# Products of zeros at the head of a conditional-residual kernel, and other planned times for its prologue

## The chip, the cores and the metric

The kernel runs on one core of a Trainium2 chip. A core has TensorE (PE in the profile; its weight loads are PEld), VectorE (DVE), ScalarE (ACT), GpSimd (POOL) and SyncE (SP), each with its own queue of instructions, and 16 DMA engines that move data between HBM and on-chip memory. All tensors are f32. The metric is the device time of one execution in microseconds, as the median of three runs.

## The reference

Four residual layers follow each other on x of shape (8, 512, 256), each with the condition cond of shape (8, 256):

```python
x = x + L0(x, cond)   # mixture of experts: a shared expert of 512, and 2 of 8 routed experts of 128
x = x + L1(x, cond)   # Haar analysis and synthesis with a gate made from cond, plus its input
x = x + L2(x, cond)   # low-rank layer; its rank-8 factors are generated from cond by W2
x = x + L3(x, cond)   # GRU over the 512 positions, then a projection
```

L0 computes `silu(x @ sw1.T) * (x @ sw3.T)` times sw2 for the shared expert, and for each routed expert `gelu(x @ rw1[e].T)` times rw2[e], weighted by gates from a sigmoid, the two best of eight scores, and a normalisation; the sum is divided by 3. L1's scales share one gate per channel, so that the layer comes down to a factor per channel and batch. L2 normalises cond, makes a hidden vector from it, and from that and W2 (8 MB) the matrices a1, b1, a2, b2. L3 takes 512 steps one after the other:

```python
Z = sigmoid(xz + H @ Whz.T + bhz);  R = sigmoid(xr + H @ Whr.T + bhr)
H = Z * H + (1 - Z) * tanh(xh + R * H @ Whh.T + bhh);  Y = H @ Whq.T + bhq
```

## The kernel before

Time is cut into 16 windows of 32 positions; a window holds 8 x 32 = 256 columns (NT). L0 to L2 of a window are matmuls of 256 columns; they run ahead of the recurrence, which then takes the window's 32 steps. Nearly all of these products go through `quads` (L485), which issues four matmuls side by side, each into its own 32 output partitions. The names of the tiles in the profile: hp and low hold hidden activations of the experts, acc their sum over experts, misc several small products, grh and gz the recurrence's gates. sw_sb, rw_sb, wsq_a and w are weights; x is the input (and, early, memory lent to pieces of W2).

Before the first step of the recurrence lies a prologue. SP's queue loads, in this order, window 0's x in two halves alternating with the two halves of sw13 (both under `load_sw13`), the rest of the first four windows' x, sw2, rw1, the square matrices, rw2, eight pieces of W2, the recurrence's weights wx and wh, and the rest of x. ACT's queue loads cond, the router and small vectors. POOL's queue loads h0 and bias rows, and fetches the broadcast gates bc from a DRAM buffer comb_d. Some engines also do the following small work: mean and variance of cond (`mean_over_features`, L833, with inv_c as stationary operand), the router's bias from cond (`time_bias`, L874), routing of four windows (`route`, L912), dense layers on cond (`dense_cond`, L1034), and the generation of the low-rank matrices (`generate`, L1104).

At the very start, DVE sets a tile `zeros`, and TensorE clears two PSUM banks with it (`claim`, L303): 8 matmuls of 256 columns for each bank. One is gz, which holds the z gate's sums.

The order of instructions is written out by hand, in two ways. In the prologue a planner, `Jobs.run`, keeps a clock for each engine. Every job has an engine, jobs that it depends on, and a planned duration `takes`; the planner goes forward in steps of 0.02 planned us, and where an engine's clock is past, emits the first job in its queue that is ready by plan. `TAKES` holds the planned defaults per engine; `load` computes `takes` of a transfer from its size in MB over RATE. These numbers produce no instruction: they only decide which job is emitted next on each engine. The jobs of windows 0 and 1 are made with the default for TensorE PE_ALONE, all later ones with PE_WOVEN. The prologue's planner stops when window 0's L0, the low-rank matrices and the recurrence's weights are there, and again once the first half of window 0 has passed L2. What of window 1 has been emitted by then is done ahead of the recurrence; the rest is woven into its steps.

In the recurrence the loop writes out each step, and `first_slot` and `second_slot` decide how many jobs of later windows are put into the step's gaps on TensorE, by how far the count of TensorE jobs left lies behind a straight line.

Of the kernel before, what the change touches and what calls it, by code (L numbers as in the profile page):

```python
# [26 lines left out]
NT = B * WS  # L27
# [4 lines left out]
NQ = 4  # L32
# [27 lines left out]
TAKES = {"PE": 0.43, "ACT": 0.4, "DVE": 0.4, "POOL": 0.8, "SP": 0.5}  # L60
PE_ALONE, PE_WOVEN = 0.43, 0.65
LEAD = 20
AHEAD = 1
RATE = 0.36
LAG = 3.5
# [72 lines left out]
class Jobs:  # L138
# [42 lines left out]
    def run(self, until):  # L181

        while any(j.done is None for j in until):
            for eng, at in self.clock.items():
                if at <= self.now:
                    qs = (self.queues[eng], self.small[eng])
                    ready = ((j, q) for q in qs for j in q if j.ready(self.now))
                    job, q = next(ready, (None, None))
                    if job is not None:
                        q.remove(job)  # L190
                        job.emit(self.now)
                        self.clock[eng] = self.now + job.takes
            self.now += 0.02

    def drain(self, now=0.0):
# [8 lines left out]
def cond_resid_kernel(  # L204
# [29 lines left out]
    nc = tc.nc  # L234
# [16 lines left out]
        for e in earlier:  # L251
            tc.declare_no_dep(later.ins, e.ins, reason="through another engine")

    TAKES["PE"] = PE_ALONE
    ctx.enter_context(tc.manual_schedule())
    const = ctx.enter_context(tc.tile_pool(name="const", bufs=1))
    dram = ctx.enter_context(tc.tile_pool(name="dram", bufs=1, space=DRAM))
# [30 lines left out]
    gz = ps_z.tile([P, 2, NG, FQ], F32, name="gz")  # L288
# [6 lines left out]
    zeros = const.tile([P, NT], F32, name="zeros")  # L295
# [3 lines left out]
    def claim(bank):  # L299

        for half in range(2):
            for j in range(NQ):
                nc.tensor.matmul(  # L303
                    bank[ts(j, 32), ts(half, NT)],
                    zeros[:, 0:32],
                    zeros,
                    start=half == 0,
                    stop=half == 1,
                    skip_group_check=True,
                )  # L310

    claim(gz.rearrange("p c n f -> p (c n f)"))
    claim(rh0)

    jobs = Jobs()
    jobs.clock["PE"] = 3.5

    def load(out, in_, mb, lazies=(), eng="SP"):

        issue = {"SP": nc.sync, "ACT": nc.scalar, "POOL": nc.gpsimd}[eng].dma_start  # L320
        return jobs.add(
            eng,
            lambda: issue(out=out.get() if isinstance(out, Lazy) else out, in_=in_),
            (),
            lazies,
            max(1.0 if eng == "POOL" else 0.45, mb / RATE),
            lag=LAG,
        )
# [46 lines left out]
    sw13_sb = const.tile([P, KC, 2, HS], F32, name="sw13_sb")  # L375
    got_sw13 = []

    def load_sw13(k):
        rows = sw13[:, ts(k, P), :].rearrange("g p h -> p g h")
        got_sw13.append(load(sw13_sb[:, k], rows, 0.5))  # L380


    load_x(0, 0.6, (0, 1), load_sw13)
    load_x(0, 0.5, (1, EARLY))
    got_vec = load(vec, vecs, 0, eng="ACT")
# [428 lines left out]
    def pe(fn, deps, lazies=(), takes=0.3):  # L814
        return jobs.add("PE", fn, deps, lazies, takes)

    def dve(fn, deps, lazies=(), takes=0.25):
        return jobs.add("DVE", fn, deps, lazies, takes)
# [4 lines left out]
    def flat(z):  # L823
        t = z.get()
        return t if len(t.shape) == 2 else t.rearrange("p a b -> p (a b)")


    def mean_over_features(src, dep):
        ps = Lazy(r_c)

        def products():
            for k in range(KC):
                nc.tensor.matmul(  # L833
                    ps.get()[:, :B], inv_c, src[:, k, :], start=(k == 0), stop=(k == KC - 1)
                )

        return ps, pe(products, [dep], [ps], 0.9)

    mu, j = mean_over_features(cond, got_cond)
    diff = set1.tile([P, KC, B], F32, name="diff")  # L840

    def center():
        for k in range(KC):
            tt(diff[:, k, :], cond[:, k, :], mu.get()[:, :B], ALU.subtract)

    j = dve(center, [j], [mu], 0.4)
    dsq = set1.tile([P, KC, B], F32, name="dsq")
    j = dve(lambda: tt(dsq, diff, diff, ALU.mult), [j])
    var_ps, j = mean_over_features(dsq, j)
    var = set1.tile([P, B], F32, name="var")  # L850
    j = dve(
        lambda: nc.vector.tensor_scalar(var, var_ps.get()[:, :B], EPS_LN, None, ALU.add),
        [j],
        [var_ps],
    )
# [5 lines left out]
    j = dve(  # L861
        lambda: tt(
            prod,
            rout[:, 1].rearrange("p k (o e) -> p k o e", o=1).broadcast_to([P, KC, B, E]),
            cond.rearrange("p k (b o) -> p k b o", o=1).broadcast_to([P, KC, B, E]),
            ALU.mult,
        ),
        [got_cond, got_rout],
    )
# [12 lines left out]
    j = pe(time_bias, [j], [tb_ps])  # L882
# [140 lines left out]
    def dense_cond(w, src, bias, name, dep):  # L1023

        ps = Lazy(r_c)
        pre = set1.tile([P, KC, B], F32, name=f"{name}_pre")

        def out(m):
            return ps.get()[:, m * B : (m + 1) * B]

        def products():
            for m in range(KC):
                for k in range(KC):
                    nc.tensor.matmul(  # L1034
                        out(m),
                        wsq_a[:, k, w, ts(m, P)],
                        src[:, k, :],
                        start=(k == 0),
                        stop=(k == KC - 1),
                    )  # L1040

        def add_bias():
            for m in range(KC):
                nc.vector.tensor_scalar(
                    pre[:, m, :], out(m), vec[:, bias, m : m + 1], None, ALU.add
                )

        j = pe(products, [dep, got_sq_a], [ps], 0.95)
        return pre, dve(add_bias, [j, got_vec], [ps], 0.4)

    def gated(pre, func, scale, name, dep):
        a = set1.tile([P, KC, B], F32, name=name)
        return a, act(lambda: nc.scalar.activation(a, pre, func, scale=scale), [dep])


    hid_pre, j = dense_cond(A_L2W1, lnc, V_BIAS1, "hid", got_lnc)
    hid_e, j = gated(hid_pre, AF.Erf, RSQRT2, "hid_e", j)
# [10 lines left out]
    g1_pre, j = dense_cond(A_L1W1, cond, V_B1, "g1", got_cond)  # L1068
    g1, j = gated(g1_pre, AF.Sigmoid, 1.0, "g1", j)
    j = dve(lambda: tt(g1, g1, g1_pre, ALU.mult), [j])  # L1070
    gate_pre, j = dense_cond(A_L1W2, g1, V_B2, "gate", j)
    gate, j = gated(gate_pre, AF.Sigmoid, 1.0, "gate", j)
# [8 lines left out]
    for n, of in enumerate(LOW):  # L1081
# [14 lines left out]
        j = pe(biased_rows, [got_b2, got_sq_a], [gp], 0.45)  # L1096
        for k in range(KC):
            got = [pieces[q, k] for q in of]

            def generate(k=k, of=of, gp=gp):  # L1100
# [12 lines left out]
            j = pe(  # L1113
                generate,
                [j, got_hid, *(g[1] for g in got)],
                [gp, *(g[0] for g in got)],
                1.75,
            )
        j = got_low_out[n] = dve(
            lambda n=n, gp=gp: nc.vector.tensor_copy(low_out[:, n], flat(gp)[:, :C]),  # L1120
            [j],
            [gp],
            0.45,
        )
# [8 lines left out]
        j = pe(turn, [j], [lt], 0.6)  # L1133
# [11 lines left out]
    l0_ends = []  # L1145

    ends = [window_jobs(w, routed, xts[w], True) for w in range(2)]
    TAKES["PE"] = PE_WOVEN

    routes = [routed]  # L1150
    for w in range(2, NW):
# [16 lines left out]
    with (  # L1168
# [145 lines left out]
        jobs.run(ends[0][0])  # L1314
        jobs.run(jobs.queues["PE"][:AHEAD])
        base = jobs.now
# [11 lines left out]
        def behind(s, by=0):  # L1328
            return (
                any(j.done is None for j in ends[1][0])  # L1330
                or jobs.left("PE") > all_left * (LAST - s) / (LAST + LEAD) + by
            )
# [29 lines left out]
        for c in range(NTC):  # L1362
            hist = hists[c]
            gates = upcoming
            for t in range(TC):
                s = c * TC + t
                n, u = t // GS, t % GS
# [194 lines left out]
```

## Time and profile before

| | us |
|---|---|
| median of three runs | 1318.25 |
| the runs | 1317.85, 1318.25, 1321.23 |
| the profiled execution | 1318.28 |
| its span, from first to last instruction | 1316.5 |
| TensorE busy | 1178.3 |
| DVE busy | 916.8 |
| ACT busy | 505.7 |
| POOL busy | 150.6 |

Busy time is the union of an engine's instructions in the span. The profile's rows give an instruction's source line, engine, operation, output and inputs; DMA-issuing instructions stand under the queue that issues them (SPq, ACTq, POOLq) and are not counted as busy. A matmul in f32 leaves two records. Idle time before an instruction stands in brackets with what ended it; it is inferred from semaphores, and where an instruction waits for several, the latest event is named. Numbers in the profile refer to the source lines of the kernel before.

### The profile page before, as it was taken

Reading aid. Unit: us, or ns where it says so; the run is one execution under the profiler, and the core shown is the slowest. Engines: PE = TensorE matmul, PEld = TensorE weight load, DVE = VectorE, ACT = ScalarE, POOL = GpSimd, SP = SyncE. Lnnn points to the kernel's source line nnn. Section 1 sums busy time; section 2 is a strip of 40 time slices with the busy share of each in tenths; the row PEclk is TensorE's granted clock in tenths of the full one; section 3 lists DMA queues with packets and bytes.
Section 4 is the critical chain, followed back from the end, with each engine's and each line's share of the span. In section 5 each row is a group of like instructions: output and inputs, shape, how many; then the busy total and the mean of one; then the engine's idle time right before and its main releaser. Section 6 shows DMA issues by size and latency. Waiting matters only on the chain.

```text
span 1316.5 us, 88999 instructions
## 1 busy us (share of the span) xinstructions
PE 1178.3 (89%) x39240; PEld 688.4 (52%) x39240; DVE 916.8 (70%) x6271; ACT 505.7 (38%) x3407; POOL 150.6 (11%) x235
## 2 busy tenths in 40 slices
PE   8999999899999999998888988888888888878886
PEld 5666555555555555555554555545554545545443
DVE  5367777777776767676776767677676767667775
ACT  2134343444344444334343433443434344433332
POOL 3311110101011110101011010101101011110000
PEclk9999999999999999999999999999999999999999
DMA  9910001200010010100000010000001000000111
GB/s 318 352 53 16 5 4 38 52 5 29 13 36 20 12 29 5 52 4 28 12 15 26 4 36 4 22 19 12 28 4 29 12 4 4 4 4 4 36 30 26
DMA packets 41859, 46.46 MB, mean 35 GB/s; under 512 B 27488, under 2 KB 31104, under 8 KB 40320
## 3 DMA queue, kind: packets, MB, share of 16 engines
q1 hardware_dynamic: 38576, 38.31, 9.5%
q8 instruction: 306, 5.01, 1.6%
q0 software_dynamic: 1184, 2.31, 0.5%
q14 instruction: 81, 0.66, 0.2%
q10 hardware_dynamic: 1712, 0.16, 0.1%
HBM read 36.45 MB, written 4.33 MB: 31 GB/s over the span
## 4 chain that ended last, share of the span: by engine, by line
PE 66%; DVE 19%; ACT 9%; issue 4%; DMA 2%; SPq 0%; ACTq 0%
PE grh L1197 35%; PE hp L485 11%; DVE d L1393 7%; DVE rT L1393 6%; PE acc L485 6%; PE gz L1197 5%; ACT c L1379 5%; PE low L485 4%; ACT r L1379 4%; PE misc L485 3%; DVE s_h L1469 3%; DVE s_rh L1410 2%; DMA bc<-comb_d 1%; DMA sw_sb<-in_sw_dram 0%; PE misc L1104 0%
## 5 line engine op out<-in xcount | busy, mean ns | idle before, releaser
L1393 DVE STREAM_TRANSPOSE rT<-r 128x32 f32<-128x32 f32 x1024 | 156.1, 191 | 219.5 <-ACT r L1379 215.8
L1379 ACT ACTIVATE r<-grh 128x32 f32<-128x32 f32 x1024 | 146.3, 195 | 421.0 <-PE grh L1197 418.2
L1197 PE MATMUL grh<-wh,s_h 128*32 128x64 f32 x8192 | 221.8, 225 | 90.1 <-DVE s_h L1469 89.1
L1197 PEld LDWEIGHTS grh<-wh,s_h 128*32 128x32 f32 x8192 | 140.4, 109 | 309.6 <-DVE s_h L1469 308.4
L1379 ACT ACTIVATE c<-grh 128x32 f32<-128x32 f32 x1024 | 146.2, 195 | 313.6 <-PE grh L1197 313.1
L1197 PE MATMUL grh<-wh,s_rh 128*32 128x64 f32 x8192 | 221.6, 225 | 34.3 <-DVE s_rh L1410 10.0
L1197 PEld LDWEIGHTS grh<-wh,s_rh 128*32 128x32 f32 x8192 | 139.2, 108 | 191.8 <-DVE s_rh L1410 188.1
L1393 DVE STREAM_TRANSPOSE d<-c 128x32 f32<-128x32 f32 x1024 | 156.5, 192 | 115.2 <-ACT c L1379 108.9
L1197 PE MATMUL gz<-wh,s_h 128*32 128x64 f32 x8192 | 209.9, 219 | 0.4 <-issue 0.3
L1197 PEld LDWEIGHTS gz<-wh,s_h 128*32 128x32 f32 x8192 | 153.5, 110 | 0.9 <-issue 0.8
L485 PE MATMUL acc<-g,rw_sb 128*32 128x256 f32 x2048 | 153.5, 379 | 0.0
L485 PE MATMUL hp<-x,sw_sb 128*32 128x256 f32 x2016 | 150.8, 384 | 2.6 <-ACT sig L583 2.2
L634 POOL TENSOR_TENSOR g<-gl,bc 128x256 f32<-128x256 f32 x128 | 93.6, 733 | 511.9 <-DVE s_h L1469 358.8
L485 PE MATMUL hp<-x,rw_sb 128*32 128x256 f32 x2016 | 151.4, 380 | 0.7 <-ACT sig L617 0.6
L1469 DVE TENSOR_TENSOR_SCAN s_h<-d,d 128x16 f32<-128x16 f32 x1024 | 145.4, 184 | 0.0
L1410 DVE TENSOR_TENSOR s_rh<-rT,s_h 128x8 f32<-128x8 f32 x1024 | 133.5, 168 | 0.0
L1393 DVE STREAM_TRANSPOSE zT<-z 128x64 f32<-128x64 f32 x512 | 121.9, 238 | 0.4 <-ACT z L1379 0.3
L1379 ACT ACTIVATE z<-gz 128x64 f32<-128x64 f32 x512 | 121.4, 237 | 0.8 <-PE gz L1197 0.4
L1483 ACT COPY hist<-s_h 128x16 f32<-128x16 f32 x512 | 106.3, 208 | 0.5 <-DVE s_h L1469 0.5
L1197 PE MATMUL grh<-wx,xt 128*32 128x128 f32 x2048 | 104.8, 274 | 1.3 <-ACT r L1379 1.1
L1422 DVE TENSOR_TENSOR d<-zT,s_h 128x16 f32<-128x16 f32 x512 | 90.7, 177 | 17.5
L1423 DVE TENSOR_SCALAR d<-zT 128x16 f32<-128x16 f32 x512 | 86.8, 169 | 0.0
(154 smaller groups left out, 1208.7 us busy)
## 6 DMA issues: line engine op xcount, KB each, us to landing
bc<-comb_d SPq DMA_DIRECT2D x56, 256.0 KB, 3.2
w<-in_w_dram SPq DMA_DIRECT2D x5, 1024.0 KB, 13.5
out_dram<-x SPq DMA_DIRECT2D x14, 256.0 KB, 3.2
x<-in_w_dram SPq DMA_DIRECT2D x3, 1024.0 KB, 15.6
x<-in_xT_dram SPq DMA_DIRECT2D x2, 1536.0 KB
bc<-comb_d POOLq DMA_DIRECT2D x8, 256.0 KB, 9.0
sw_sb<-in_sw_dram SPq DMA_DIRECT2D x3, 512.0 KB, 8.0
wsq_a<-in_sq_a_dram SPq DMA_DIRECT2D x1, 1280.0 KB
```

Source lines behind the costliest of these rows:

```text
L485: nc.tensor.matmul(out[ts(j, 32)], lhs[:, ts(j, 32)], rhs, start=start, stop=False, skip_group_check=True,)
L634: lambda gl=gl, g=g, e=e: nc.gpsimd.tensor_tensor(g.get(), gl.get(), bcs[e // 2].get()[:, e % 2], ALU.mult),
L1197: nc.tensor.matmul(out[ts(j, 32)], lhs, rhs[:, ..., ts(j, FQ)], start=start, stop=False, skip_group_check=True,)
L1379: nc.scalar.activation(x, y, func)
L1393: ins = nc.vector.transpose(dst.rearrange("p i u b -> p i (u b)"), src.rearrange("p (i r) -> p i r", r=32),)
L1410: prod = tt(s_rh[u][:, k, u, :], rT[:, k, u, :], h[:, k], ALU.mult)
L1422: tt(d1[:, :, u, :, 1], zT[:, :, u, :], h, ALU.mult)
L1423: nc.vector.tensor_scalar(d0[:, :, :, 1], zT[:, :, u, :], -1.0, 1.0, ALU.mult, ALU.add)
L1469: new = nc.vector.tensor_tensor_scan(s_h[v][:, k, v].rearrange("p b w -> p (b w)"), d0[:, k].rearrange("p b w -> p (b w)"), d1[:, k, u].re ...
L1483: nc.scalar.copy(hist[:, :, t, :], s_h[v][:, :, v, :, 1])
```

## The change

A constant `WARM` of 10.0 planned us is added. While a planned clock is below it, and TensorE's clock is past with no ready job, the planner calls `self.idle()`, which emits four matmuls of zeros, 128 columns wide, into gz (with start and stop off, so they add to the bank that `claim` cleared), and advances TensorE's clock by its default. `add_zeros` takes the place of that call. The planned default of DVE in the prologue becomes 0.45, and goes back to 0.4 when window 1's jobs have been made; each half of sw13 is planned as 0.55 MB in place of 0.5. One added line sets TensorE's clock to 4.0, and the line behind it, which was there, sets it to 3.5.

```diff
+WARM = 10.0
@@ Jobs.run
                         job.emit(self.now)
                         self.clock[eng] = self.now + job.takes
+                    elif eng == "PE" and self.now < WARM:
+                        self.idle()
+                        self.clock[eng] = self.now + TAKES[eng]
@@ cond_resid_kernel
-    TAKES["PE"] = PE_ALONE
+    TAKES["PE"], TAKES["DVE"] = PE_ALONE, 0.45
...
+    def add_zeros():
+        for j in range(NQ):
+            nc.tensor.matmul(
+                gz.rearrange("p c n f -> p (c n f)")[ts(j, 32), : NT // 2],
+                zeros[:, 0:32],
+                zeros[:, : NT // 2],
+                start=False,
+                stop=False,
+                skip_group_check=True,
+            )
...
     jobs = Jobs()
+    jobs.idle = add_zeros
+
+    jobs.clock["PE"] = 4.0
     jobs.clock["PE"] = 3.5
...
-        got_sw13.append(load(sw13_sb[:, k], rows, 0.5))
+        got_sw13.append(load(sw13_sb[:, k], rows, 0.55))
...
     ends = [window_jobs(w, routed, xts[w], True) for w in range(2)]
-    TAKES["PE"] = PE_WOVEN
+    TAKES["PE"], TAKES["DVE"] = PE_WOVEN, 0.4
```

## The prediction

> **What bounds the kernel now.** I read the page first, for the whole; then TensorE's instructions in order of time through the prologue; then narrow stretches; then the waits.
>
> ```profile
> span 1316.5 us, 88999 instructions
> PE 1178.3 (89%) x39240; PEld 688.4 (52%) x39240; DVE 916.8 (70%) x6271; ACT 505.7 (38%) x3407; POOL 150.6 (11%) x235
> ...
> PE 66%; DVE 19%; ACT 9%; issue 4%; DMA 2%; SPq 0%; ACTq 0%
> ```
>
> Two stages make the span. The recurrence of 512 steps begins with its first product of the state, at 67.16 us below, and takes the rest, 1316.5 - 67.2 = 1249.3 us, 2.44 us a step. The scans (L1469) stand at 40 to 42 pairs in every 100 us, with three groups of woven products in half of the steps (early) or a fifth of them (late): the step's own chain of products, gates and transposes sets its pace. So what the change can move is when that first product starts.
>
> ```profile
> 1.19 1.94 PE L303 MATMUL gz<-zeros 128*32 128x256 f32 x16 [1.19 <-DVE zeros L296]
> 2.90 1.93 PE L303 MATMUL grh<-zeros 128*32 128x256 f32 x16
> 4.76 1.02 PE L833 MATMUL grh<-cond,inv_c 128*128 128x8 f32 x4
> 6.12 1.12 PE L874 MATMUL grh<-prod,ones 128*128 128x64 f32 x4 [0.33 <-DVE diff L844]
> 7.60 1.08 PE L485 MATMUL hp<-x,sw_sb 128*32 128x256 f32 x8 [0.36 <-DMA sw_sb<-in_sw_dram]
> 8.61 1.02 PE L833 MATMUL grh<-dsq,inv_c 128*128 128x8 f32 x4
> 9.56 2.79 PE L485 MATMUL hp<-x,sw_sb 128*32 128x256 f32 x24
> ...
> 16.68 0.64 PE L485 MATMUL low<-x,sw_sb 128*32 128x256 f32 x8 [0.51 <-ACT sig L583]
> 17.13 1.05 PE L912 MATMUL grh<-x,rout_sq 128*32 128x256 f32 x16
> 17.99 0.61 PE L485 MATMUL hp<-x,sw_sb 128*32 128x256 f32 x8
> 18.43 1.05 PE L485 MATMUL acc<-g,sw_sb 128*32 128x256 f32 x16
> ...
> 67.16 0.43 PE L1197 MATMUL grh<-wh,s_h 128*32 128x64 f32 x16
> ```
>
> These are TensorE's instructions in time (start, length, count of records; a matmul leaves two records, and four matmuls side by side, eight records, are one "group"). Idle time stands in brackets. From 7.60 us to the loop TensorE idles a few times, by 0.2 to 1.1 us each: the prologue is bound by TensorE's work, and DMA keeps just ahead of it. Now the same kind of group at two speeds, in stretches of 1 us (length, busy and records, granted clock, DMA share, GB/s):
>
> ```profile
> 12.00:13.00 1.00, 1.00 (x16) 1.00 1.02 320
> 13.00:14.00 1.00, 1.00 (x16) 1.00 1.16 399
> 14.00:15.00 1.00, 1.00 (x25) 1.00 1.13 344
> ```
>
> Sixteen records fit into 1 us until 14 us, and 25 after: a group costs 0.86 us before and 0.43 us after (17.99 to 18.43 above). In quarter microseconds the turn lies at about 13.9 us. The column of the granted clock says 1.00 throughout, so this slow state is read from the records' pace alone. From 7.60 to 13.9 TensorE works 6.3 us at half speed, and a fast one would need 3.15 us.
>
> **The head under the change.** Built, the new program holds three calls of add_zeros: four matmuls of 128 columns after the claims, eight between the mean (L833) and the variance product (L833, of dsq). No others: later the planner always finds work. Half as many columns as the claims' groups (0.86 us each, slow) make an estimated 0.43 us a call. Slow throughout, the head runs: claims to 4.8, zeros to 5.25, mean (1.0 us as in its row) to 6.25, zeros to 7.1. The variance product, formerly behind the first group of hp, stands ahead of it and takes to 8.05, 0.45 us of it past the 7.60 at which hp could start; the time-bias product (L874), formerly hidden before 7.6, stands among the hp groups. Work ahead of the first data costs nothing: it lies beside the transfer of sw_sb that ends at 7.46. If that transfer were early, it would cost up to the 1.3 us of the three calls.
>
> **Does it open the clock?** The row: slow from 1.19 to 13.9. [...]
>
> **Sum with the clock open at 7.1.** Variance product: four records, at the fast price of 0.12 us each (L1034's eight records of 128x8 take 0.99 us), to 7.6. Two groups of hp 0.86, time bias 0.5, four groups 1.72: 10.7. The second half of sw_sb was issued at 2.78 and landed 8.0 us later, 10.8, so no wait of note. Six groups 2.6, one group of hp and the routing pair (L912) 1.3: 14.7. In before the same work ends at 18.43. Lead 3.7 us: 3.2 of clock and the 0.51 us that low waited for ACT at 16.68, which the new order (n=0 and n=1 back to back) doesn't wait.
> With the clock shut: 8.05, two groups 1.72, time bias 1.0, 3.6 slow groups to 13.9, then fast: 18.0; lead 0.4.
>
> **Behind the head.** VectorE's planned 0.45 and the load's 0.55 only move instructions (takes is no instruction). No queue of SP or POOL changes its order, and no DMA is added. On TensorE two stalls of 0.57 us on ACT's reads of a bank go (16.68, counted, and 20.90), and two of 0.56 come: hp_5 and hp_8 now have their last group straight behind the group that ACT reads, where a dense product and L1104 stood. Net +0.55. Two more groups of window 1 stand ahead of the loop (one hp of rw_sb, one acc), 0.86 us on TensorE's path, with two fewer in it. There they lay in the step's slack; from steps of (half of three groups) 2.43 and (a fifth) 2.40 us a group costs about 0.1, so the relief is 0.2. Net +0.65. The positions of some tens of other groups in the loop shift by a step; counts of steps with one, two and three groups agree within a few, so 0, at most 0.5 either way.
> Transfers: with TensorE 3 us earlier, each product moved must still find its data. L1104 at 35.09 needs a piece landed at 30.1 (issued 13.5, 16.6 to land), slack 5; at 46.73 one landed at 40.6, slack 6; the fifth w piece waits for TensorE itself and follows it:
>
> ```profile
> SPq L323 <- PE misc L1104: 8.0, 1, 8.0
> SPq L323 <- DMA wsq_a<-in_sq_a_dram: 7.2, 1, 7.2
> ...
> POOL g L634 <- DMA bc<-comb_d: 5.9, 2, 4.5
> ```
>
> SP's own row says when wsq_a landed: 22.36, where SP goes on; its first use at 26.13 moves to about 23. bc lands at 40.9, and its product on POOL (0.73) is wanted at 43.20: slack 1.5, unless routing, VectorE's chain and the comb_d transfer, which all start from L912, move along, as they should. I allow 0.3 for these (bounds 0 and 2.2: all slack lost). First gate of the loop: ACT's idle of 2.8 us is named after bc, but the built instruction waits only for pieces and comb_d writes landed earlier and for the product at 67.16; 0.1 us is all it is late.
> Sum: -3.7 + 0.55 + 0.65 + 0.3 = -2.2. From the profiled execution's 1318.28 (span 1316.5 and 1.8 around it): **1316.1**.
>
> **Rivals.**
> [...]
> The clock opens and the transfers eat it: bc's landing stays at 40.9 because it shares the DMA engines (busy 0.95 or more from 10 to 50 us) with w pieces, so the first rw acc stays at 41.65 at the earliest, 1.5 us before the old one; -1.5 + 1.2 = -0.3, and with wsq_a or sw2 late none: 1318.0. For it: L634's 4.5 us wait. Against: bc was issued only at 34.2, after comb_d.
> The loop's changed order decides, by its few displaced groups or an instruction fetch such as the 1.2 us of "issue" before 70.53: +-0.5 ordinarily, and over 4 us only if it repeated in several steps, which the equal counts don't suggest.
>
> **How the numbers follow.** 0.3% is 3.95 us, about what a measurement of this kernel can tell from no change (the three runs spread 0.26%). Clock open, full gain 0.50 (1316.1, own range 1314.3 to 1317.6); open but eaten 0.20 (1318.0); shut 0.20 (1319.1, 1318.3 to 1320.3); the loop's order 0.10, half either way (1313 or 1323). Faster by 0.3% needs 1314.3: a tenth of the first, a few of the others, and half of the last: 0.14. Slower needs 1322.2: half of the last and tails: 0.09. Range from the first's low tail to the third's high: 1313.9 to 1320.5.
>
> **What would show it.** Right: groups of hp at 0.43 us from about 7.6; L912 near 14; the rw acc near 40; first product of the state near 65; 1249 us after it. Wrong: 0.86 us groups to 13 or 14; TensorE idle before L1104, L1034 or acc with a DMA or POOL named; a start unmoved; or a start moved with a longer loop.

## The result, and the profile after

The changed kernel took 1322.19 us (median of 11 runs, 1318.40 to 1326.02), the kernel before 1318.25 (11 runs, 1316.79 to 1321.31): 1.0025 of it, interval 1.0015 to 1.0035. The forecast was 1316.1 within 1313.9 to 1320.5, so it was wrong in sign and outside its range. The profiled execution took 1324.59 us, 2.4 above the median, while that of before (1318.28) lies at its median: what follows splits the 6 us between these two executions, not the 3.9 between the medians. Its page begins so (span; busy time of each engine; shares of the chain that ended last; one row of the DMA queues):

```profile
span 1322.5 us, 89028 instructions
PE 1181.6 (89%) x39264; PEld 690.8 (52%) x39264; DVE 917.5 (69%) x6271; ACT 505.7 (38%) x3407; POOL 150.5 (11%) x235
...
q8 instruction: 306, 5.01, 1.5%
...
PE 67%; DVE 19%; ACT 9%; issue 4%; ACTq 0%; DVEq 0%
```

TensorE has 24 records more than before (39,264 against 39,240): the 12 matmuls of zeros. The row of queue 8 was not used in the prediction and matters below: 306 packets, 5.01 MB, so 16.4 KB each; TensorE's 39,264 + 39,264 records over 306 packets are 257 a packet.

TensorE in order of time, after (start, length, records; idle time in brackets):

```profile
4.61 0.66 PE L321 MATMUL gz<-zeros 128*32 128x128 f32 x8
5.20 1.02 PE L852 MATMUL grh<-cond,inv_c 128*128 128x8 f32 x4
6.15 1.08 PE L321 MATMUL gz<-zeros 128*32 128x128 f32 x16
7.16 1.02 PE L852 MATMUL grh<-dsq,inv_c 128*128 128x8 f32 x4
8.12 1.94 PE L504 MATMUL hp<-x,sw_sb 128*32 128x256 f32 x16
9.98 1.12 PE L893 MATMUL grh<-prod,ones 128*128 128x64 f32 x4
...
17.20 1.04 PE L931 MATMUL grh<-x,rout_sq 128*32 128x256 f32 x16
18.06 0.61 PE L504 MATMUL hp<-x,sw_sb 128*32 128x256 f32 x8
...
68.70 0.22 PE L1216 MATMUL grh<-wh,s_h 128*32 128x64 f32 x1
...
72.28 0.80 PE L504 MATMUL low<-x,wsq_a 128*32 128x128 f32 x9 [2.61 <-issue]
72.71 0.68 PE L1216 MATMUL grh<-wh,s_rh 128*32 128x64 f32 x15
```

The zeros stand where they were expected and hp starts at 8.12, but its groups still cost 0.86 us: the array stayed slow. The same stretches as shown of before say the same (16 records in 1 us until 14 us):

```profile
12.00:13.00 1.00, 1.00 (x16) 1.00 1.02 323
13.00:14.00 1.00, 1.00 (x16) 1.00 1.06 373
14.00:15.00 1.00, 1.00 (x24) 1.00 1.08 324
```

So the routing product stands at 17.20 (17.13 before), and the first product of the state at 68.70 (67.16), 1.54 us late. Then comes a wait of 2.61 us of a kind that the page calls "issue": TensorE waits for nothing that the profile shows. ScalarE's activation of z, once a step, counts the loop. Before, and then after, the first two:

```profile
67.94 0.23 ACT L1379 ACTIVATE z<-gz 128x64 f32<-128x64 f32 x1
71.78 0.24 ACT L1379 ACTIVATE z<-gz 128x64 f32<-128x64 f32 x1
```

```profile
69.59 0.23 ACT L1398 ACTIVATE z<-gz 128x64 f32<-128x64 f32 x1
75.85 0.24 ACT L1398 ACTIVATE z<-gz 128x64 f32<-128x64 f32 x1
```

The step between them takes 3.84 us before and 6.26 after; an undisturbed one takes 2.42 in both. The last z is 6.00 us later than in before, of which 1.65 are there at the first z, 2.42 come in this step, and 1.93 in the other 510. The tail is the same. TensorE's "issue" waits from 62 us on (total, times, longest), before and after:

```profile
PE low L485 <- issue: 1.2, 1, 1.2
PE grh L1197 <- issue: 1.1, 2, 0.9
PE gz L1197 <- issue: 0.3, 1, 0.3
```

```profile
PE low L504 <- issue: 2.6, 1, 2.6
PE gz L1216 <- issue: 2.2, 5, 0.8
PE hp L504 <- issue: 0.4, 1, 0.4
PE grh L1216 <- issue: 0.2, 1, 0.2
```

They are 2.6 us before and 5.4 after. The 1.20 that the prediction passed over as a possible instruction fetch is the first of them.

### The profile page after: what moved, and what is told of

It is laid out like the page before. It is cut to its first block, busy times and chain, and to the rows that moved or that the text cites. A ratio compares the mean times of both kernels' runs of the same rounds, so it can differ in the third digit from the quotient of the medians.

```text
span 1322.5 us, 89028 instructions
## 1 busy us (share of the span) xinstructions
PE 1181.6 (89%) x39264; PEld 690.8 (52%) x39264; DVE 917.5 (69%) x6271; ACT 505.7 (38%) x3407; POOL 150.5 (11%) x235
## 3 DMA queue, kind: packets, MB, share of 16 engines
q8 instruction: 306, 5.01, 1.5%
## 4 chain that ended last, share of the span: by engine, by line
PE 67%; DVE 19%; ACT 9%; issue 4%; ACTq 0%; DVEq 0%
PE grh L1216 35%; PE hp L504 11%; DVE d L1412 7%; DVE rT L1412 6%; PE acc L504 6%; PE gz L1216 5%; ACT c L1398 5%; PE low L504 5%; ACT r L1398 4%; PE misc L504 4%; DVE s_h L1488 3%; DVE s_rh L1429 2%; PE misc L1123 1%; ACT sig L602 0%; PE grh L1053 0%
## 6 DMA issues: line engine op xcount, KB each, us to landing
x<-in_w_dram SPq DMA_DIRECT2D x3, 1024.0 KB, 14.7
```

## What the waits are

Three readings of the two traces suggested it. First, the place. Counted from the start of the kernel, this gap stands behind the same record of TensorE, the 1111th, in both traces, although the changed program has other instructions there: in before the end of step 0's second woven product, in after the middle of its first, 40 records earlier in the program. The other gaps stand 127 records ahead of it or nearly whole multiples of 128 behind it (a few records are missing from the traces). With 257 records of TensorE a packet, near 128 matmuls and 128 weight loads, I take the place for the end of a block of instructions which one packet of queue 8 brings.

Second, the time of the packet. In the trace's record of queue 8 the packet for this block starts at 68.08 us before and at 69.99 after, and TensorE goes on 2.45 and 2.29 us later. Elsewhere in the loop it mostly starts while 80 to 120 records of the block ahead are still to come (about eight packets in ten), here with 31 left (before) and none (after).

Third, what it waits behind. In stretches of 1 us, the last of 2 us (length, TensorE's busy time and records, granted clock, DMA share, GB/s), before and then after:

```profile
66.00:67.00 1.00, 0.83 (x40) 1.00 1.04 398
67.00:68.00 1.00, 1.00 (x67) 1.00 0.88 338
68.00:69.00 1.00, 0.78 (x39) 1.00 0.34 121
69.00:70.00 1.00, 0.33 (x13) 1.00 0.04 14
```

```profile
67.00:68.00 1.00, 1.00 (x49) 1.00 1.06 405
68.00:69.00 1.00, 1.00 (x63) 1.00 0.89 340
69.00:70.00 1.00, 0.67 (x39) 1.00 0.39 141
70.00:71.00 1.00, 0.00 (x0) 1.00 0.12 45
...
72.00:74.00 2.00, 1.72 (x43) 0.50 0.03 8
```

The last load of x (3 MB for windows 4 to 15) keeps the DMA engines full until about 68 and 69, and the packet of instructions starts as it ends. The last row shows the price on top: after 2.6 us without work the clock was granted at 0.50, and about 3 us of work ran at half speed (until about 75.3).

The theory to test was then: the change's loss comes from where these blocks end, not from the zeros' work or the order. Its 12 matmuls make TensorE's stream 48 instructions longer ahead of the loop, and its two groups more ahead of the loop add to that until the loop, which holds two groups fewer, has evened them out. Every block in the loop then ends at another place in a step and is fetched at another time. Rivals: the zeros' own work at the head; the order that the new planned times give; the bulk load alone.

## Experiments

In the tables "stream" is the count of TensorE's matmuls against the kernel before. Each set shares its chip and its runs of the kernel before.

**The parts of the change, one by one.**

e1_idle_alone: the calls of zeros alone, with the planned times of before.

```diff
-    TAKES["PE"], TAKES["DVE"] = PE_ALONE, 0.45
+    TAKES["PE"], TAKES["DVE"] = PE_ALONE, 0.4
...
-        got_sw13.append(load(sw13_sb[:, k], rows, 0.55))
+        got_sw13.append(load(sw13_sb[:, k], rows, 0.5))
```

> The kernel before plus the calls of add_zeros alone (planned 0.4 for VectorE and 0.5 MB for sw13 kept): the three calls of zeros and the new order at the head, but no extra groups ahead of the loop. Theory A (TensorE runs out of fetched instructions at the loop's start while bulk loads hold the DMA engines, and the clock doesn't open earlier): clock opens at about 13.9 us as before, first product of the state within 0.6 us of the 67.2 of before, but the end of the fetched block lies 24 records earlier in the program, so the stall after step 0 is about 2 us instead of 1.2: 0.5 to 2.5 us slower than before. Theory B (the two extra groups and stalls ahead of the loop make the loss, zeros cost nothing): within 0.5 us of before. Theory C (zeros open the clock in most runs and only the profiled run of the changed kernel missed it): 2 to 3 us faster.

e2_dve_alone: VectorE's planned 0.45 alone, no zeros, the load at 0.5.

```diff
-WARM = 10.0
+WARM = 0.0
...
-        got_sw13.append(load(sw13_sb[:, k], rows, 0.55))
+        got_sw13.append(load(sw13_sb[:, k], rows, 0.5))
```

> The kernel before with VectorE planned at 0.45 in the prologue alone: no zeros, two more groups of window 1 ahead of the loop. Theory A: the loop starts 0.9 to 1.4 us later than in before, the block's end lies 16 records earlier and the bulk loads end later, so the stall grows too: 1.5 to 3.5 us slower. Theory B: 1 to 1.5 us slower, with the stall unchanged at 1.2 us. Theory C: 0.5 to 1.5 us slower.

e3_no_zeros: the order of the changed kernel; a call of idle emits nothing.

```diff
-    jobs.idle = add_zeros
+    jobs.idle = lambda: None
```

> The changed kernel with add_zeros emitting nothing while the planner counts its time: same order as the changed kernel, without the 12 matmuls of zeros. Theory A: the clock opens at the same edge as with them, near 13.9; the block's end moves 24 records later than in the changed kernel, so the stall at the loop's start shrinks from 2.6 us towards 1.5: 1 to 2.5 us faster than the changed kernel's 1322.2, that is 1319.7 to 1321.2. Theory B: within 0.5 us of the changed kernel. If the zeros themselves delay the mean and what follows: up to 0.7 us faster.

e4_dense: the kernel before, with 12 matmuls of zeros of 256 columns straight behind the claims, so that TensorE streams without a gap from 1.2 to 7 us.

```diff
     claim(rh0)
+    for _ in range(3):
+        for j in range(NQ):
+            nc.tensor.matmul(
+                gz.rearrange("p c n f -> p (c n f)")[ts(j, 32), :NT],
+                zeros[:, 0:32],
+                zeros,
+                start=False,
+                stop=False,
+                skip_group_check=True,
+            )
```

> The kernel before with three more groups of zeros, 256 columns wide, right behind the claims (12 matmuls as in the changed kernel, but back to back, to about 7.3 us), planner untouched. [...] If zeros as operands don't count at all: the clock opens at 13.8 and it is 0.5 to 1.5 us slower.

| | stream | us | ratio, interval |
|---|---|---|---|
| before (39 runs) | 0 | 1319.33 | |
| e1_idle_alone | +12 | 1321.09 | 1.0014, 1.0005 to 1.0022 |
| e2_dve_alone | 0 | 1319.81 | 1.0004, 0.9995 to 1.0014 |
| e3_no_zeros | 0 | 1320.11 | 1.0005, 0.9996 to 1.0013 |
| e4_dense | +12 | 1320.90 | 1.0012, 1.0002 to 1.0021 |

The order alone (e2, e3) makes no difference that shows in the time, though its profiles have the long wait too; each has two groups (8 matmuls) more ahead of the loop. The two with 12 matmuls more are slower, whatever they contain.

The long wait in step 0 isn't what sets these two apart: it is 2.14 us in e2, 2.67 in e3, 1.85 in e1 and 2.13 in e4. The traces part behind it. From 76 us on the "issue" waits of a profile sum to about 2.0 us in e1 and in e4 and 2.8 in the changed kernel's first profile, to 1.2 in before, and to 0.6 and 0.4 in e2 and e3. In all five profiles of kernels with 12 matmuls more (these three, e5 and e7 below) TensorE waits 0.3 to 0.6 us behind its record 8790 and 0.4 to 0.5 behind 16086 (around steps 98 and 194). Of the nine other profiles only e11's has a wait at the first place (0.25), and none has one at the second.

In e4 the clock was open (groups at the fast pace) by the time of hp: its first group, at 7.72 us, took 0.64 us as the fast ones do (1.08 in before), and the first z came 1.00 us earlier than in before. It was then lost in step 0 (granted at 0.50 from 70 to 73 us), in the view of TensorE in time:

```profile
69.90 0.53 PE L1207 MATMUL grh<-wh,s_rh 128*32 128x64 f32 x9 [2.13 <-issue]
```

So in this execution the opened clock didn't pay for itself. In e1 the first zeros already run fast (0.39 us, 0.66 in the changed kernel's first profile), behind nothing but the claims, and hp, which comes behind a wait of 1.08 us for sw_sb, is slow again (16 records in 1.83 us, 1.07 in e5 below). TensorE in time:

```profile
4.54 0.39 PE L321 MATMUL gz<-zeros 128*32 128x128 f32 x8
7.70 1.83 PE L504 MATMUL hp<-x,sw_sb 128*32 128x256 f32 x16 [1.08 <-DMA sw_sb<-in_sw_dram]
```

So in e1 the clock was open before any zeros were added, and the three calls of them didn't keep it open. What this set can't say is whether the 12 matmuls cost by their work or by their number.

**The same zeros in fewer instructions.**

e5_after_again is the changed kernel, run beside the next three.

> The changed kernel, unaltered, beside the next three on one chip. All theories: about 1.0025 of before again. If theory A is right, the profile shows a stall of 2 us or more after step 0, and the same slow steps 98, 130, 132, 194 and 199 as in the changed kernel's first profile and in the two experiments with 12 matmuls more (idle alone, dense); edges of the clock may lie elsewhere.

e6_after_aligned: the changed kernel, with each four matmuls of zeros side by side written as one over all 128 columns of the array, and the second half of rh0's claim written so too. The same columns are streamed in 12 matmuls less, so that the stream has the length of before.

```diff
-        for j in range(NQ):
-            nc.tensor.matmul(
-                gz.rearrange("p c n f -> p (c n f)")[ts(j, 32), : NT // 2],
-                zeros[:, 0:32],
+        nc.tensor.matmul(
+            gz.rearrange("p c n f -> p (c n f)")[:, : NT // 2],
+            zeros[:, 0:P],
...
-    claim(rh0)
+    for j in range(NQ):
+        nc.tensor.matmul(
+            rh0[ts(j, 32), ts(0, NT)],
+            zeros[:, 0:32],
+            zeros,
+            start=True,
...
+    nc.tensor.matmul(
+        rh0[:, ts(1, NT)],
+        zeros[:, 0:P],
+        zeros,
+        start=False,
+        stop=True,
...
```

> The changed kernel with the same zeros written in fewer instructions: each call is one matmul 128 columns of weights wide in place of four of 32, and the last quarter of the claims likewise, so that the stream ahead of the loop holds as many matmuls as without add_zeros and the loop stands at the place in the fetched blocks that it has in before. Theory A (where the blocks end decides): slow steps 98, 130, 132, 194 and 199 vanish; 1.5 to 2.5 us faster than the changed kernel, like the version that emits no zeros (1.0005 of before). Theory Z (the work of zeros itself costs, by delaying the head): no gain over the changed kernel, 1.002 to 1.003.

e7_after_late_x: the changed kernel, with the last 3 MB of x cut into twelve loads of 256 KB, one in every second step of the loop.

```diff
-    load_x(NW - EARLY, 1.8)
+    late_x = []
+    xg.append((EARLY * WS, x_rest))
+    xw.extend(x_rest[:, :, :, ts(i, WS)] for i in range(NW - EARLY))
+    for i in range((NW - EARLY) // 2):
+        at = ts(i, 2 * WS)
+        got = [
+            jobs.add(
+                "SP",
+                lambda k=k, at=at, i=i: nc.sync.dma_start(
+                    out=x_rest[:, k, :, at],
+                    in_=xs[:, k, :, (EARLY + 2 * i) * WS : (EARLY + 2 * i + 2) * WS],
+                ),
+                takes=0.7,
+                queue={"SP": late_x},
+                lag=LAG,
+            )
+            for k in range(KC)
+        ]
+        got_x.extend([got] * 2)
...
                 jobs.fill("SP", now, 1)
+                if s >= 2 and s % 2 == 0:
+                    jobs.fill("SP", now, 1, of=[late_x])
```

> The changed kernel with its last bulk load (x of windows 4 to 15, 3 MB) cut into twelve loads of 256 KB, issued one every second step from step 2 on. Theory A: when the loop starts no bulk load holds the DMA engines, TensorE's next block of instructions is there in time; no stall after step 0, step 1 takes under 3.5 us in place of 6.3, the clock stays open: 2.5 to 4 us faster than the changed kernel. Theory B (the stall has another cause, a wait on a semaphore or a table load): step 1 is as slow as before, and the time is the changed kernel's within 1 us.

e8_before_late_x: the same in the kernel before.

> The kernel before with the same late loads. Theory A: its stall of 1.2 to 1.5 us after step 0 goes; 1 to 2 us faster than before. Theory B: same as before within 0.7 us. If the late loads delay fetches within the loop instead: slow steps between 2 and 26, and the gain is lost.

| | stream | us | ratio, interval |
|---|---|---|---|
| before (33 runs) | 0 | 1319.90 | |
| e5_after_again | +12 | 1324.85 | 1.0032, 1.0020 to 1.0044 |
| e6_after_aligned | 0 | 1319.66 | 1.0001, 0.9992 to 1.0009 |
| e7_after_late_x | +12 | 1324.92 | 1.0032, 1.0021 to 1.0044 |
| e8_before_late_x | 0 | 1322.61 | 1.0020, 1.0011 to 1.0029 |

e6 against e5 is the decisive pair: the same columns of zeros and the same planned times, 12 matmuls less, and 5.2 us come back, all that the change had cost. Its "issue" waits are 3.0 us instead of 7.2 (e5's profile), none of them longer than 1.3:

```profile
PE grh L1231 <- issue: 2.1, 2, 1.3
PE gz L1231 <- issue: 0.9, 1, 0.9
```

e5 tells of the clock. In its profiled execution it was open when hp began: its 16 records at 7.66 took 1.07 us, and the routing product stands at 14.02, where the prediction had it. The kernel took 1325.92 us all the same. TensorE in time:

```profile
7.66 1.07 PE L504 MATMUL hp<-x,sw_sb 128*32 128x256 f32 x16 [0.44 <-DMA sw_sb<-in_sw_dram]
...
14.02 1.35 PE L931 MATMUL grh<-x,rout_sq 128*32 128x256 f32 x13
...
16.77 1.07 PE L504 MATMUL acc<-g,sw_sb 128*32 128x256 f32 x16 [0.76 <-DMA sw_sb<-in_sw_dram]
...
66.82 0.22 PE L1216 MATMUL grh<-wh,s_h 128*32 128x64 f32 x1
...
70.67 0.80 PE L504 MATMUL low<-x,wsq_a 128*32 128x128 f32 x9 [2.88 <-issue]
```

Of 3.18 us that the routing product is earlier than in the first profile of this kernel (17.20), 1.88 are left at the first product of the state; 0.76 went to the third piece of sw_sb (sw2), which is not there yet. The block of instructions then held step 0 up by 2.88 us.

e7 and e8 took the bulk load away from step 0. The long wait went (step 0 to 1 takes 2.72 and 2.51 us, from 6.26 and 3.84 in the first profiles), so it does hang on that load. But the time did not fall, and before became slower: while the small loads run, steps 10 to 28 hold new waits. e7's:

```profile
PE gz L1234 <- issue: 2.6, 4, 1.0
PE grh L1234 <- issue: 2.0, 4, 0.8
PE acc L522 <- issue: 0.9, 1, 0.9
```

With loads of 256 KB TensorE waits as well, for up to 1.0 us here and 1.85 in e8 (before step 14, at 102.60 us), and more often: from 62 us on e7 has 11 "issue" waits and the changed kernel's first profile 8, e8 has 12 and before 4. As a remedy this failed.

**The length of the stream alone.** If only the place of the blocks matters, it must work in the kernel before too, in both directions.

e9_dense_same_length is e4 with its zeros and rh0's second half in matmuls over all 128 columns:

```diff
+    for _ in range(3):
+        nc.tensor.matmul(
+            gz.rearrange("p c n f -> p (c n f)")[:, :NT],
+            zeros[:, 0:P],
+            zeros,
+            start=False,
+            stop=False,
+            skip_group_check=True,
+        )
```

> The kernel before with 256-column zeros behind the claims (as in e4), but in three matmuls over all 128 columns of the array instead of twelve over 32, and three of rh0's claims saved the same way, so that TensorE's instruction stream is as long as in the kernel before. Late blocks of instructions: the slow steps 98, 130, 194 and 199 of e4 are absent, 2 to 3 us come back against e4; the loop starts about 1.0 us earlier than before when the clock opens at 5, and the block in step 0, which still waits for the end of the x load near 68 us, holds step 1 up by those 1.0 us more: in all 0 to -0.5 against before, about 1319. Work of the zeros itself: as e4, +1.0 to +1.6.

e10_shift_back is before with the 16 matmuls of both claims written as 4, with nothing added:

```diff
-    claim(gz.rearrange("p c n f -> p (c n f)"))
-    claim(rh0)
+    for tile in (gz.rearrange("p c n f -> p (c n f)"), rh0):
+        for n in range(2):
+            nc.tensor.matmul(
+                tile[:, ts(n, NT)],
+                zeros[:, 0:P],
+                zeros,
+                start=n == 0,
+                stop=n == 1,
+                skip_group_check=True,
+            )
```

> The kernel before with the 16 matmuls of the two claims written as 4 over all 128 columns: the same columns streamed, no zeros added, the order as before; the stream is 12 matmuls (48 instructions) shorter, so every block ends 12 matmuls, about 0.8 us of the loop, later in the program. Late blocks of instructions: the wait in step 0 falls from 1.2 to about 0.4 us, step 1 by about 0.8, and the later slow steps are others than before's step 60; total -0.5 to -2 if no new ones come, up to +2 if they do. Any other cause: nothing changes, within 0.3 us step by step.

e11_after_shift_back is the changed kernel with those claims and e6's zeros:

> The changed kernel with its zeros in 3 matmuls instead of 12 and both claims in 4 instead of 16: 21 matmuls fewer than the changed kernel, 9 fewer than before. Late blocks of instructions: step 0's wait at most 1 us instead of 2.6, no slow steps 98, 130, 194 and 199 unless this third position brings its own; 1318 to 1321, below the changed kernel by 3 to 6. Work of the zeros or the order of the groups: near the changed kernel, 1324 to 1325.

e12_dense_shift_back is e10 with four of e9's matmuls of zeros behind the claims:

> The kernel before with four 128-column matmuls of zeros of 256 columns behind the claims and the claims in 4 matmuls: 8 matmuls fewer than before, the clock open at about 5. Late blocks of instructions: the loop starts 1.0 us earlier, step 0's wait is 1.2 + 1.0 - 0.5 = 1.7 us, in all about -0.5 against before if no new slow steps come. If the early clock were worth its whole 3.2 us, -2 or more.

| | stream | us | ratio, interval |
|---|---|---|---|
| before (38 runs) | 0 | 1319.73 | |
| e9_dense_same_length | 0 | 1318.43 | 0.9992, 0.9984 to 1.0000 |
| e10_shift_back | -12 | 1318.45 | 0.9988, 0.9980 to 0.9996 |
| e11_after_shift_back | -9 | 1319.20 | 0.9994, 0.9986 to 1.0002 |
| e12_dense_shift_back | -8 | 1316.87 | 0.9976, 0.9966 to 0.9985 |

e9 against e4 repeats the pair of e5 and e6 without any of the change's order: the same columns of zeros in 12 matmuls less take it from 1.0012 to 0.9992 of before. In e10 nothing is added or reordered, and the time moves too, by an amount that its interval just tells from none. e11 stays slow until 14 us (hp's groups at 0.86, routing at 17.08, hardly earlier than the changed kernel's) and yet is 0.3 to 0.4% faster than it (0.9994 of before, against 1.0025 and 1.0032). Where the blocks end thus decides the change's loss, and not the clock or the zeros.

The details of my expectations missed. In e9 and e10 I expected the wait in step 0 to move; it changed its block. e10's two waits in TensorE's time:

```profile
67.89 0.32 PE L1205 MATMUL gz<-wx,xt 128*32 128x64 f32 x8 [1.58 <-issue]
...
71.91 0.24 PE L1205 MATMUL grh<-wh,s_h 128*32 128x64 f32 x1 [0.63 <-issue]
```

The first is the end of the block ahead of the 1111th record, behind the 984th: its packet started at 65.27, not at 63.60 as in before, and held up the input products ahead of the loop; why the packet started later isn't shown. So one can't count in advance on what a shift brings.

e12 is the best version found, 2.9 us below before. Its clock is open when hp begins (0.64 us for the first group, 1.08 in before), and it pays for that 1.03 us in hp's start, 8.63 instead of 7.60; TensorE in time:

```profile
4.77 2.60 PE L324 MATMUL gz<-zeros 128*128 128x256 f32 x8
...
8.63 0.64 PE L503 MATMUL hp<-x,sw_sb 128*32 128x256 f32 x8
...
66.16 0.42 PE L1215 MATMUL grh<-wx,xt 128*32 128x128 f32 x8 [1.81 <-issue]
...
70.29 0.36 PE L1215 MATMUL grh<-wh,s_h 128*32 128x64 f32 x9 [0.62 <-issue]
```

It still waits 1.81 us for a block just ahead of the loop, but its second z comes 0.83 us earlier than before's and its other 510 steps take 0.95 us less. Whether the 1.6 us between e10 and e12 come from the clock or from the place of the blocks isn't shown. It was found by trying four lengths, and a change anywhere in the prologue can undo it.

## Why the prediction was wrong

**What it got right.** The three calls of zeros, their place (4.61 and 6.15), hp after 8.05 (8.12) and the zeros' cost at nothing ahead of sw_sb held. So did the case "shut" as far as the first product of the state: with the lead at the routing product at -0.07 instead of 0.4, net 0.55 for ACT's stalls and 0.86 for the two groups (whose relief of 0.2 lies in the loop), it comes to 1.48 us late, and 1.54 was measured in this execution (in e5 the first product came 0.34 us earlier than in before). The stalls were as named: those of 16.68 and 20.90 are gone, two of 0.56 stand at 32.06 and 41.63. VectorE's planned time only moves work (e2: 1.0004). One slip in the sum decides nothing: the head comes to 14.6 (10.7 + 2.6 + 1.3), not 14.7, and the lead to 3.8.

**The step on the clock.** The sum has the clock open at 7.1, and from this a lead of 3.7 us. No run shows a turn at 7.1: in the profiled execution the array stayed slow from 7.1 to about 13.9 (groups of hp at 0.86 us) with no gap from 4.6 on; in e5, the same program, the second call's zeros at 6.00 were already fast (16 records in 0.64 us, against 1.08), and hp at 7.66 too. In e1 it was fast from about 4.5, ahead of the added zeros, and slow again at hp (1.83 us for 16 records). So neither "it opens at 7.1" nor "it doesn't" is a property of the program, and the turn at 13.9 in one trace should not have been used as fixed. What sets the turn isn't shown. The step's other half failed as well: in e5 the gain of 3.18 us at the routing product had shrunk to 1.88 by the loop, 0.76 of it in the wait for sw2, which the sum has at nothing and only a rival names ("with wsq_a or sw2 late").

**The step on the loop** decided the sign. The sum has nothing for the loop, "at most 0.5 either way". It said of the displaced instructions and the "issue" of 1.2 us: "over 4 us only if it repeated in several steps, which the equal counts don't suggest". Equal counts of woven groups say nothing about it. What counts is how many instructions stand ahead of a point of the loop, and that had changed by 12 matmuls of zeros and two groups. In the profiled execution the wait for the first late block grew from 1.20 to 2.61 us and the clock closed, 2.42 us in all for that step, and the other steps, with the later waits, added 1.93. Since e2 and e3 have the long first wait too, and no loss clear of noise, the zeros' own share lies in good part in the later waits. The zeros were costed at nothing because work hides their time; their number was not costed.

**Which part is shown, and which open.** That the loss goes with the number of instructions is shown by e5 and e6 (1.0032 and 1.0001), and by e4 and e9 (1.0012 and 0.9992), where the work stays and the number changes. That the wait in step 0 hangs on the last x load is shown by e7 and e8 (step 0 to 1 in 2.72 and 2.51 us). That the later waits are fetches behind loads is argued from the traces: of the changed kernel's six of 0.3 us or more behind step 0, five have a packet that starts within 0.3 us of the end of a transfer of 256 KB (at 387.81 us for the wait that ends at 390.34), and one, ending at 394.91, has no such transfer ahead of its packet. None was tested singly. Single profiles of one kernel differ by some 2 us through the clock and these waits (e5 and the first profile of the changed kernel agree in step 0 but not in the rest: +4.19 and +1.93), so the split of a total by one profile is good to no better than that. Why 12 matmuls more cost 1.6 us in e4, and the whole change 3.9 to 5.0, isn't settled beyond the latter's two groups.

## What to carry to other kernels

In this program, 89,028 instructions written out without a loop, the instructions themselves were a stream of transfers (306 packets, 5.01 MB). In one like it, read the "issue" waits and the instruction queue beside the bulk loads, and count what an edit adds ahead of the tight part, even where its time is hidden. Filler work should come in as few instructions as possible (one matmul over 128 columns, not four over 32: 12 matmuls less took 5.2 us off from e5 to e6). A change of some 0.2% that shifts the stream has to be compared with a version that has the same length before its idea is judged.

## What the runs showed that was not expected

- At the loop's start TensorE waited 1.20 us in before and 2.61 in the changed kernel's first profile for a packet of instructions (16.4 KB) that started as the last load of x (340 to 400 GB/s) ended, and 2.88 at the same place in e5. With loads of 256 KB the longest wait was still 1.85 us (e8).
- After the wait of 2.61 us the clock was granted at 0.50 from 72 to 74 us, and groups took twice their time until about 75.3. The length of a wait alone doesn't tell: behind e9's wait of 2.05 us the pace fell too, at about 67.8 us (granted 0.63 from 67 to 70), while behind e3's of 2.67 us it stayed fast (0.62 us for the group at 72.59).
- The column of the granted clock reads 1.00 during the first slow stretch; only the pace of the records shows it (16 in 1 us, then 24).
